# Layer 0 of a four-layer graph network: gathered rows in three bf16 parts, one-hot sums in bf16, gathers released four tiles at a time

## The chip, the cores and the metric

The kernel runs on one core of one Trainium2 chip. The metric is the device time of one run in microseconds (us), as the median of several runs. Besides the runs there is one execution under the hardware profiler, from which the page and the trace come.

## The reference

There are 8192 nodes with 32 features each and 262144 edges sorted by their target node `dst`. Four layers follow one another, and after each the node features are replaced by the layer norm of features plus layer output. The change concerns layer 0:

```python
w_e   = jnp.take(weight, etypes, axis=0)        # one of 64 matrices of 32x32 per edge
h_src = jnp.take(feat, src, axis=0)
msg   = jnp.einsum('ei,eio->eo', h_src, w_e)
out   = jax.ops.segment_sum(msg, dst, num_segments=8192)
```

Layer 1 sums `x[src] * edge_weight` over the edges of each target, layer 2 sums `x[src]`, and layer 3 makes a message from each edge's features with a small two-layer network and sums those.

## The kernel before

The edges stand in 2048 tiles (TT) of 128 edges, one edge per partition. Eight tiles (GT) make a group, so there are 256 groups (GG). Because the edges are sorted, the targets of one group fall into a window of 128 nodes; `rel` holds each edge's place in that window.

A first phase multiplies every node's features by all 64 matrices and writes the products to a table in DRAM, `ytab` (in the trace `fytab`), with 8192 x 64 rows of 32 numbers. The message of an edge is then one row of that table. While this phase runs, VectorE counts degrees and GpSimd fetches 64 records per node group, which `slots()` later turns into the tables `meta_l`, `meta_k` and `meta_w`.

The main loop of layer 0 does two independent things, interleaved in an order that is written out by hand. Each engine takes its own instructions strictly in the order of the program and waits only for the marks named in `after(...)`; `now(PE)` is the last mark that TensorE has been given so far.

The first thing is layer 0 itself. For group g:

- `gathers` (line 423) lets GpSimd issue one indirect DMA per tile (line 380 of the profile). It brings 128 rows of 32 f32 numbers from `ytab` into `xg`, which holds four slabs of 32 tiles. It is called once per slab of four groups. Before each group it waits until the sums that last read that place of `xg`, 16 groups back, are done (`taken`), and until the second last group of gathers has landed (`LAG`).
- `one_hot` (line 502) lets VectorE compare `rel` with an iota in PSUM, which gives an f32 matrix of 128 x 128 per tile in `oh` (four buffers).
- Eight f32 products on TensorE (line 605) sum the eight tiles into 32 columns of a PSUM bank; the profile shows each f32 product as two records. When 16 groups have filled a bank, ScalarE copies it to `win` (line 610).
- When enough of `win` is there, `windows` (line 492) shifts and adds the overlapping windows of eight node blocks on TensorE, and `normalize` (lines 451 to 461) does the layer norm on VectorE and ScalarE. This happens eight times.

The second thing is `matrices(i)`, 256 units that prepare layers 1 and 2. From group 8 on, group g is followed by one unit, sometimes by two. In a unit VectorE builds one-hot matrices (lines 554, 556, 559; `w_ps` in PSUM holds edge weights, refreshed by line 552), TensorE multiplies them in four quarters q0 to q3 of eight f32 products each (line 568), ScalarE evicts each quarter (lines 572 and 573), and SyncE stores 1 MB to `amat` and 0.5 MB to `cmat` (lines 577 and 578). VectorE's one-hot matrices have two buffers, so it starts unit i when q3 of unit i-2 is done.

Before group 4 the loop waits for `slots()`, whose transposes (line 530) run on TensorE and whose evictions (line 534) run on ScalarE.

Layer 1 begins when the last unit and the last normalization of layer 0 are done (line 643 loads `amat`). Layer 3 gathers too, from another table (`fxtab`), and there GpSimd is let go four tiles at a time, by the products of line 860.

Of the kernel before, what the change touches and what calls it, by code (L numbers as in the profile page):

```python
# [13 lines left out]
BF = mybir.dt.bfloat16  # L14
# [131 lines left out]
def raw_layers(tc, x, a, w0, w1, b1, w2, si, m, bad):  # L146
# [34 lines left out]
    def now(f):  # L181
        return (f.sem, f.n)
# [16 lines left out]
    st_c = cut(2, 4, 2, 256, dt=BF)  # L199

    xg = cut(4, WT, D)
    oh = cut(4, GT, P)
    win = cut(GG, D)
    end0 = cut.at

# [22 lines left out]
    hi_b = digits[:, 0:TT // 2].bitcast(BF)  # L228
    lo_b = digits[:, TT // 2:TT].bitcast(BF)
    iota = bank[:, 7, 0:P]  # L230
    w_ps = bank[:, 7, P:P + 384]


    dsti = rel.bitcast(I32)
# [210 lines left out]
    def normalize(l, c, acc, pm, x_in, x_out, x3=None):  # L445


        ds = slice(c * LC, (c + 1) * LC)
        y, yc, sq = (lnf[:, k].rearrange("p (d f) -> p d f", f=D) for k in range(3))
        V.after(pm, ln_last[0])  # L450
        read = own(V, V.e.tensor_add(y, acc.rearrange("p (d f) -> p d f", f=D), x_in[:, ds, :]))
        own(V, V.e.tensor_reduce(lns[:, 0], y, AX.X, OP.add))
        own(V, V.e.tensor_scalar(lns[:, 1], lns[:, 0], 1.0 / D, None, op0=OP.mult))
        vm = V.mark(V.e.tensor_sub(yc, y, lns[:, 1, :, None].to_broadcast([P, LC, D])))
        A.after(vm)
        V.after(A.mark(A.e.activation(sq, yc, AF.Square)))
        A.after(V.mark(V.e.tensor_reduce(lns[:, 2], sq, AX.X, OP.add)))
        V.after(A.mark(A.e.activation(lns[:, 0], lns[:, 2], AF.Sqrt, bias=eps, scale=1.0 / D)))
        own(V, V.e.reciprocal(lns[:, 3], lns[:, 0]))
        xo = x_out[:, ds, :]  # L460
        ln_last[0] = V.mark(V.e.tensor_tensor(xo, yc, lns[:, 3, :, None].to_broadcast([P, LC, D]), op=OP.mult))
        if x3 is not None:

            r1, r2 = y, sq
            V.after(ln_last[0])
            own(V, V.e.tensor_copy(x3[:, ds, 0:D], xo))
            own(V, V.e.tensor_sub(r1, xo, x3[:, ds, 0:D]))
            own(V, V.e.tensor_copy(x3[:, ds, D:2 * D], r1))
            own(V, V.e.tensor_sub(r2, r1, x3[:, ds, D:2 * D]))
            ln_last[0] = V.mark(V.e.tensor_copy(x3[:, ds, 2 * D:], r2))  # L470
        if l == 2:
            S.after(ln_last[0])
            x_st.add(S.e.dma_start(xtab.rearrange("(d p) f -> p d f", p=P)[:, ds, :], xo))
        return read

    def windows(c, acc, free):

        d0 = c * LC
        todo = []
        for j in [0, 1, 2, 3, -2, -1, 4]:  # L480
# [64 lines left out]
    def matrices(i):  # L545

        b, pp, k0 = i % 2, i // 2, 16 * (i % 2)
        WB = 24
        if i % WB == 0:
            n = min(WB * 16, CB * 16 - i * 16)  # L550
            V.after(now(V))
            own(V, V.e.tensor_copy(w_ps[:, 0:n], meta_w.rearrange("p n k -> p (n k)")[:, i * 16:i * 16 + n]))
        V.after(oh_used[b])
        own(V, V.e.tensor_tensor(oh_k[:, b, :, 0, :], iota[:, None, 0:64].to_broadcast([P, 16, 64]),  # L554
                                 meta_k[:, pp, k0:k0 + 16, None].to_broadcast([P, 16, 64]), op=OP.is_equal))
        V.e.tensor_tensor(oh_l[:, b], iota[:, None, :].to_broadcast([P, 16, P]),  # L556
                          meta_l[:, pp, k0:k0 + 16, None].to_broadcast([P, 16, P]), op=OP.is_equal)
        wo = (i % WB) * 16
        vm = V.mark(V.e.tensor_tensor(oh_k[:, b, :, 1, :], oh_k[:, b, :, 0, :],
                                      w_ps[:, wo:wo + 16, None].to_broadcast([P, 16, 64]), op=OP.mult))  # L560
        PE.after(vm)
        for q in range(4):
            bk = 3 + 2 * (units[0] % 2)
            PE.after(bank_free[units[0] % 2])
            for j in range(4):
                for h in range(2):
                    hs_ = slice(64 * h, 64 * h + 64)
                    ins = PE.e.matmul(bank[:, bk + h, :].rearrange("p (c s j) -> p c s j", s=64, j=4)[:, :, :, j],  # L568
                                      oh_l[hs_, b, 4 * q + j, :], oh_k[hs_, b, 4 * q + j], start=True, stop=True)
            pm = PE.mark(ins)  # L570
            A.after(pm, st_ld[b].mark() if q == 0 and st_ld[b].n else None)
            A.e.activation(st_c[:, b, q], bank[:, bk:bk + 2, 0:256], AF.Copy)  # L572
            bank_free[units[0] % 2] = am = A.mark(A.e.activation(st_a[:, b, q], bank[:, bk:bk + 2, 256:512], AF.Copy))  # L573
            units[0] += 1
        oh_used[b] = pm
        S.after(am)
        st_ld[b].add(S.e.dma_start(amat[:, 2048 * i:2048 * (i + 1)], st_a[:, b].rearrange("p u h c -> p (u h c)")))
        st_ld[b].add(S.e.dma_start(cmat[:, 2048 * i:2048 * (i + 1)], st_c[:, b].rearrange("p u h c -> p (u h c)")))
# [10 lines left out]
    FIRST = 8  # L589
    made = 0  # L590
    done = 0
    per = 512 // D
    for g in range(GG):
        s, h, bk, c = g * GT // WT, g % NO, (g // per) % 2, g % per
        if g == FIRST // 2:
            V.after(slots(), x_in)
        if g * GT % WT == 0:
            k, landed = gathers(ytab, row, s)
        V.after(oh_free[h])
        om = V.mark(one_hot(oh[:, h], g * GT, GT))  # L600
        PE.after(landed[g % 4], om)
        if c == 0:
            PE.after(agg_free[bk])
        for t in range(GT):
            ins = PE.e.matmul(bank[:, bk, c * D:(c + 1) * D], oh[:, h, t, :], xg[:, k, g * GT % WT + t, :],  # L605
                              start=(t == 0), stop=(t == GT - 1))
        oh_free[h] = taken[k][g % 4] = pm = PE.mark(ins)
        if c == per - 1:
            A.after(pm)
            agg_free[bk] = am = A.mark(A.e.activation(win[:, g + 1 - per:g + 1, :].rearrange("p g f -> p (g f)"),  # L610
                                                      bank[:, bk, :], AF.Copy))
            while done < NB // LC and ready(done) <= g + 1:
                pm = windows(done, bank[:, 2, 0:LC * D], (acc_free[0], am))
                acc_free[0] = normalize(0, done, bank[:, 2, 0:LC * D], pm, x_a, x_b)
                done += 1
        if g >= FIRST:
            upto = min(CB, (g - FIRST + 1) * CB // (GG - FIRST - 4))
            while made < upto:
                matrices(made)
                made += 1  # L620
    stored = [ld.mark() for ld in st_ld]


# [140 lines left out]
    def fetch_rows(q):  # L764

        if q < NQ:
            G.after(quad.get(q - AHEAD, {}).get("w"))
            rows[q // 8] = gathers(xtab, src, q // 8, q % 8 * 4, 4)
# [640 lines left out]
```

## Time and profile before

| | |
|---|---|
| median of 3 runs | 7803.98 us (7796.38 to 7807.71) |
| profiled execution | 7682.45 us, span 7680.7 us |
| TensorE busy (matmuls), weight loads | 76%, 55% of the span |
| VectorE, ScalarE, GpSimd busy | 49%, 22%, 52% |
| granted TensorE clock, mean | 0.792 |
| first phase | until about 272 us, where the gathers of layer 0 begin |
| layer 0's loop with units | 605 to 3593 us (first and last store of `amat`) |
| layers 1 and 2 | about 3611 to 4600 us |
| layer 3 | about 4600 to 7680 us |

The trace's times count from the span's start. In its rows a name left of `<-` is written, those right of it are read; `x8` means eight instructions merged into one row, and the brackets at the end give the engine's idle time just before and what is taken to have ended it. "remote" and "issue" are waits whose releaser the profile does not show. DMA-issuing time of SyncE stands under SPq.

### The profile page before, as it was taken

How to read it: one execution, taken by the hardware profiler on the slowest of the kernel's cores; microseconds unless marked ns; L12 is line 12 of the kernel's file. 1: busy time of each engine (PE TensorE's matmuls, PEld its weight loads, DVE VectorE, ACT ScalarE, POOL GpSimd, SP SyncE). 2: the span in 40 equal slices, each digit the busy share in tenths (PEclk: the TensorE clock that was granted, in tenths of full speed). 3: DMA queues.
4: the chain of work that ended last, by engine and by line, in shares of the span. 5: the costliest groups of instructions: out<-in, count | busy, mean ns of one | idle time of the engine just before them, and what ended most of it. 6: DMA issues, size and time to landing. Idle time of an engine off the chain costs nothing.

```text
span 7680.7 us, 88486 instructions
## 1 busy us (share of the span) xinstructions
PE 5868.9 (76%) x36084; PEld 4261.6 (55%) x36084; DVE 3758.9 (49%) x6691; ACT 1653.0 (22%) x2828; POOL 4001.1 (52%) x4174
## 2 busy tenths in 40 slices
PE   5327777787877778786444776989898889888898
PEld 2116767776767667676222344555555555555555
DVE  3304444444444454544000004666666766676666
ACT  3123333333333333333000001111111111111111
POOL 3456656565656656561000006666666666666663
PEclk7556777777777777777777887999999899999999
DMA  8405655555555555567999981111111111111111
GB/s 285 144 10 125 144 141 143 142 145 140 143 142 145 148 134 151 136 149 217 432 432 429 403 336 26 24 24 24 24 24 27 24 24 24 24 24 24 24 24 19
DMA packets 290736, 999.46 MB, mean 130 GB/s; under 512 B 99022, under 2 KB 175887, under 8 KB 250639
## 3 DMA queue, kind: packets, MB, share of 16 engines
q1 hardware_dynamic: 155742, 916.89, 33.0%
q0 software_dynamic: 134144, 73.67, 9.4%
q8 instruction: 286, 4.69, 0.3%
q10 hardware_dynamic: 432, 3.15, 0.1%
q14 instruction: 132, 1.07, 0.1%
HBM read 521.39 MB, written 471.99 MB: 129 GB/s over the span
## 4 chain that ended last, share of the span: by engine, by line
PE 51%; DVE 15%; another core or an unknown queue 15%; DMA 10%; issue 6%; ACT 3%; SPq 0%; DVEq 0%; ACTq 0%
PE bank L869 16%; PE bank L568 15%; PE bank L860 9%; DMA f_arena<-famat 6%; PE bank L605 3%; PE bank L836 3%; DMA f_arena<-fcmat 3%; DVE f_arena L904 3%; DVE f_arena L502 2%; DVE f_arena L556 2%; PE bank L684 2%; PE bank L687 2%; DVE f_arena L900 2%; ACT f_arena L573 1%
## 5 line engine op out<-in xcount | busy, mean ns | idle before, releaser
L380 POOL DMA_INDIRECT f_arena<-fxtab,f_src x2048 | 1971.8, 963 | 2135.8 <-DVE f_arena L740 1111.0
L380 POOL DMA_INDIRECT f_arena<-fytab,f_row x2048 | 1962.0, 958 | 1338.6 <-issue 552.8
L568 PE MATMUL bank<-f_arena 64*128 64x128 f32 x16384 | 1846.0, 376 | 580.1 <-issue 416.2
L568 PEld LDWEIGHTS bank<-f_arena 64*128 64x128 f32 x16384 | 1619.5, 275 | 792.3 <-issue 572.6
L869 PE MATMUL bank<-f_arena 128*128 128x344 f32 x4096 | 1486.7, 511 | 288.6 <-DVE f_arena L502 284.2
L869 PEld LDWEIGHTS bank<-f_arena 128*128 128x128 f32 x4096 | 860.2, 214 | 764.2 <-DVE f_arena L502 348.7
L572 ACT ACTIVATE f_arena<-bank 128x512 bf16<-128x512 f32 x1024 | 612.3, 598 | 1886.7 <-remote 1163.8
L860 PE MATMUL bank<-f_arena 65*128 65x256 f32 x4096 | 1005.2, 388 | 0.0
L554 DVE TENSOR_TENSOR f_arena<-bank,f_arena 128x1024 f32<-128x1024 f32 x256 | 313.3, 1224 | 1363.4 <-remote 1281.6
L860 PEld LDWEIGHTS bank<-f_arena 65*128 65x128 f32 x4096 | 762.5, 191 | 357.3 <-issue 223.0
L844 ACT ACTIVATE f_arena<-bank,f_arena 64x512 f32<-64x512 f32 x512 | 351.1, 686 | 2530.8 <-PE bank L836 909.5
L502 DVE TENSOR_TENSOR f_arena<-bank,f_rel 128x512 f32<-128x512 f32 (+1 forms) x768 | 659.1, 859 | 246.1 <-ACT f_arena L534 233.6
L605 PE MATMUL bank<-f_arena 128*128 128x32 f32 x4096 | 545.3, 283 | 125.4 <-DMA f_arena<-fytab,f_row 69.0
L573 ACT ACTIVATE f_arena<-bank 128x512 f32<-128x512 f32 x1024 | 607.7, 593 | 0.0
L605 PEld LDWEIGHTS bank<-f_arena 128*128 128x128 f32 x4096 | 509.8, 199 | 155.2 <-issue 107.3
L556 DVE TENSOR_TENSOR f_arena<-bank,f_arena 128x2048 f32<-128x2048 f32 x256 | 586.6, 2291 | 8.8
L904 DVE TENSOR_TENSOR f_arena<-bank,f_arena 128x256 f32<-128x256 f32 x1536 | 551.3, 415 | 0.0
L684 PE MATMUL bank<-f_arena,f_x_b 128*32 128x256 f32 x4096 | 293.9, 458 | 335.5 <-DMA f_arena<-famat 335.5
L897 DVE TENSOR_TENSOR f_arena<-bank,f_arena 128x256 f32<-128x256 f32 x512 | 215.9, 422 | 660.8 <-PE bank L860 288.0
L684 PEld LDWEIGHTS bank<-f_arena,f_x_b 128*32 128x32 f32 x4096 | 145.5, 131 | 472.6 <-DMA f_arena<-famat 309.8
L900 DVE TENSOR_TENSOR f_arena<-bank,f_arena 128x512 f32<-128x512 f32 x512 | 348.8, 681 | 0.0
L687 PE MATMUL bank<-f_arena 128*96 128x512 bf16 x1024 | 248.7, 405 | 80.1 <-DMA f_arena<-fcmat 80.1
(127 smaller groups left out, 2628.1 us busy)
## 6 DMA issues: line engine op xcount, KB each, us to landing
famat<-f_arena SPq DMA_DIRECT2D x256, 1024.0 KB
fcmat<-f_arena SPq DMA_DIRECT2D x256, 512.0 KB
fytab<-f_arena SPq DMA_DIRECT2D x64, 1024.0 KB
f_arena<-fytab,f_row POOLq DMA_INDIRECT x2048
f_arena<-fxtab,f_src POOLq DMA_INDIRECT x2048
f_arena<-laid_ea SPq DMA_DIRECT2D x64, 512.0 KB
f_arena<-laid_ea SPq DMA_DIRECT2D x64, 64.0 KB
f_arena<-laid_xT ACTq DMA_DIRECT2D x1, 1024.0 KB, 8.0
```

The costliest lines, as they stand in the source:

```text
L380: return G.e.indirect_dma_start(out=dest, out_offset=None, in_=table, in_offset=bass.IndirectOffsetOnAxis(ap=ix, axis=0))
L502: return V.e.tensor_tensor(o, iota[:, None, :].to_broadcast([P, n, P]), rel[:, t:t + n, None].to_broadcast([P, n, P]), op=OP.is_equal)
L556: V.e.tensor_tensor(oh_l[:, b], iota[:, None, :].to_broadcast([P, 16, P]), meta_l[:, pp, k0:k0 + 16, None].to_broadcast([P, 16, P]), op=OP ...
L568: ins = PE.e.matmul(bank[:, bk + h, :].rearrange("p (c s j) -> p c s j", s=64, j=4)[:, :, :, j], oh_l[hs_, b, 4 * q + j, :], oh_k[hs_, b, ...
L572: A.e.activation(st_c[:, b, q], bank[:, bk:bk + 2, 0:256], AF.Copy)
L573: bank_free[units[0] % 2] = am = A.mark(A.e.activation(st_a[:, b, q], bank[:, bk:bk + 2, 256:512], AF.Copy))
L605: ins = PE.e.matmul(bank[:, bk, c * D:(c + 1) * D], oh[:, h, t, :], xg[:, k, g * GT % WT + t, :], start=(t == 0), stop=(t == GT - 1))
L684: ins = PE.e.matmul(bank[q * D:(q + 1) * D, b, 0:256].rearrange("p (u h j) -> p u h j", h=2, j=4), x_b[:, s, :], mv[:, s], start=(s < 4), ...
L860: ins = PE.e.matmul(wp[:, t, :], hs[0:65, q % 4, t * P:(t + 1) * P], w2_s[0:65], start=True, stop=True)
L869: ins = PE.e.matmul(bank[:, g % 2, 0:MW], oh[:, c % NO, t, :], p[:, c % NP, t, :], start=(c % 2 == 0 and t == 0), stop=(c % 2 == 1 and t = ...
L900: V.e.tensor_tensor(pq[:, :, 0:128].rearrange("p t (o k) -> p t o k", k=16), wp[:, :, 0:128].rearrange("p t (o k) -> p t o k", k=16), a0[: ...
L904: V.e.tensor_tensor(pq[:, :, 128 + 64 * mm:192 + 64 * mm].rearrange("p t (o i) -> p t o i", i=8), wp[:, :, 192:256].rearrange("p t (o i) - ...
```

## The change

- The one-hot matrices `oh` are written in bf16.
- A new function `parts(g)` lets VectorE split the f32 rows of a group in three bf16 parts. It masks the upper 16 bits into PSUM (`x_ps`, which takes room from `w_ps`), converts them to bf16, subtracts, and does this again for the remainder. It is six instructions on 128 x 256 numbers. It waits for the landing of the group's gathers; `taken` is now marked by its first subtraction.
- TensorE multiplies each bf16 one-hot with the 96 columns of the three parts. A PSUM bank now takes four groups, and VectorE (`bank_out`) adds the three parts of each into `win`, two groups later than before; ScalarE's copy is gone.
- Gathers are issued in halves of four tiles by `fetch_rows`. Twelve groups are issued ahead of the loop. After that, the first half of group g+12 waits for the sums of group g, and the second half for the last TensorE mark after the units of group g.
- `w_ps` is refreshed every 8 units instead of every 24.

```diff
-    oh = cut(4, GT, P)
+    oh = cut(4, GT, P, dt=BF)
+    xp = cut(4, GT, 3, D, dt=BF)
+    xr = cut(2, GT * D)
...
-    w_ps = bank[:, 7, P:P + 384]
+    w_ps = bank[:, 7, P:2 * P]
+    x_ps = bank[:, 7, 2 * P:2 * P + GT * D]
...
-        WB = 24
+        WB = 8
...
+    def fetch_rows(g, h, let):
+        if g < GG:
+            G.after(let)
+            gathers(ytab, row, g * GT // WT, g * GT % WT + h * GT // 2, GT // 2)
+            if h == 1:
+                landed[g] = under_way[-1]
+    def parts(g):
+        k, t0, u = g * GT // WT % 4, g * GT % WT, g % 4
+        xv = xg[:, k, t0:t0 + GT, :].rearrange("p t f -> p (t f)")
+        r = xr[:, g % 2]
+        pi = x_ps.bitcast(I32)
...
+        V.after(landed[g], prev_parts[0])
+        own(V, V.e.tensor_scalar(pi, xv.bitcast(I32), upper16, None, op0=OP.bitwise_and))
+        V.e.tensor_copy(part[0], tf(x_ps))
+        taken[k][g % 4] = own(V, V.e.tensor_tensor(r, xv, x_ps, op=OP.subtract))
+        own(V, V.e.tensor_scalar(pi, r.bitcast(I32), upper16, None, op0=OP.bitwise_and))
+        V.e.tensor_copy(part[1], tf(x_ps))
+        prev_parts[0] = V.mark(V.e.tensor_tensor(part[2], tf(r), tf(x_ps), op=OP.subtract))
+        return prev_parts[0]
+    def bank_out(n):
+        V.after(sums_of[per * n + per - 1])
+        agg_free[n % 2] = vm = V.mark(V.e.tensor_reduce(
+            win[:, per * n:per * (n + 1), :], bank[:, n % 2, 0:per * 3 * D].rearrange("p (g c f) -> p g f c", c=3, f=D),
+            AX.X, OP.add))
+        return vm
...
+    for g in range(AHEAD):
+        for h in range(2):
+            fetch_rows(g, h, None)
+    for g in range(GG + 2):
+        if g >= 2 and (g - 2) % per == per - 1:
+            vm = bank_out((g - 2) // per)
+            while done < NB // LC and ready(done) <= g - 1:
...
-        if g * GT % WT == 0:
-            k, landed = gathers(ytab, row, s)
         V.after(oh_free[h])
-        om = V.mark(one_hot(oh[:, h], g * GT, GT))
-        PE.after(landed[g % 4], om)
+        one_hot(oh[:, h], g * GT, GT)
+        PE.after(parts(g))
...
-            ins = PE.e.matmul(bank[:, bk, c * D:(c + 1) * D], oh[:, h, t, :], xg[:, k, g * GT % WT + t, :],
-                              start=(t == 0), stop=(t == GT - 1))
-        oh_free[h] = taken[k][g % 4] = pm = PE.mark(ins)
-        if c == per - 1:
-            A.after(pm)
-            agg_free[bk] = am = A.mark(A.e.activation(win[:, g + 1 - per:g + 1, :].rearrange("p g f -> p (g f)"),
-                                                      bank[:, bk, :], AF.Copy))
...
+            ins = PE.e.matmul(bank[:, bk, 3 * c * D:3 * (c + 1) * D], oh[:, h, t, :],
+                              xp[:, g % 4, t].rearrange("p c f -> p (c f)"), start=(t == 0), stop=(t == GT - 1))
+        oh_free[h] = sums_of[g] = PE.mark(ins)
+        fetch_rows(g + AHEAD, 0, sums_of[g])
         if g >= FIRST:
...
                 matrices(made)
                 made += 1
+        fetch_rows(g + AHEAD, 1, now(PE))
```

More of the change, by code (lines that the diff above doesn't have):

```diff
@@ L591, in raw_layers @@
     done = 0
-    per = 512 // D
-    for g in range(GG):
-        s, h, bk, c = g * GT // WT, g % NO, (g // per) % 2, g % per
+    per = 4
+    AHEAD = 12
+    landed = {}
+    sums_of = {}
+    made_at = [None]
+    upper16 = -65536
+    def fetch_rows(g, h, let):
[9 more added lines that the diff above has]
+        pi = x_ps.bitcast(I32)
+        part = [xp[:, u, :, c, :] for c in range(3)]
+        tf = lambda v: v.rearrange("p (t f) -> p t f", f=D)
+        V.after(landed[g], prev_parts[0])
[6 more added lines that the diff above has]
+        return prev_parts[0]
@@ new lines, in bank_out @@
+    def bank_out(n):
[4 more added lines that the diff above has]
+        return vm
+    prev_parts = [None]
+    for g in range(AHEAD):
[5 more added lines that the diff above has]
+            while done < NB // LC and ready(done) <= g - 1:
+                pm = windows(done, bank[:, 2, 0:LC * D], (acc_free[0], vm))
+                acc_free[0] = normalize(0, done, bank[:, 2, 0:LC * D], pm, x_a, x_b)
+                done += 1
+        if g >= GG:
+            continue
+        h, bk, c = g % NO, (g // per) % 2, g % per
@@ L604, in raw_layers @@
         for t in range(GT):
-            ins = PE.e.matmul(bank[:, bk, c * D:(c + 1) * D], oh[:, h, t, :], xg[:, k, g * GT % WT + t, :],
-                              start=(t == 0), stop=(t == GT - 1))
-        oh_free[h] = taken[k][g % 4] = pm = PE.mark(ins)
-        if c == per - 1:
-            A.after(pm)
-            agg_free[bk] = am = A.mark(A.e.activation(win[:, g + 1 - per:g + 1, :].rearrange("p g f -> p (g f)"),
-                                                      bank[:, bk, :], AF.Copy))
[L612 to L615, printed above, removed]
+            ins = PE.e.matmul(bank[:, bk, 3 * c * D:3 * (c + 1) * D], oh[:, h, t, :],
+                              xp[:, g % 4, t].rearrange("p c f -> p (c f)"), start=(t == 0), stop=(t == GT - 1))
+        oh_free[h] = sums_of[g] = PE.mark(ins)
+        fetch_rows(g + AHEAD, 0, sums_of[g])
         if g >= FIRST:
```

## The prediction

> **What bounds the kernel now.** The page first: TensorE is the busiest engine, and the two gathers (L380) are the longest rows; the one into f_row's table (fytab) is layer 0's.
>
> ```profile
> PE 5868.9 (76%) x36084; PEld 4261.6 (55%) x36084; DVE 3758.9 (49%) x6691; ACT 1653.0 (22%) x2828; POOL 4001.1 (52%) x4174
> L380 POOL DMA_INDIRECT f_arena<-fytab,f_row x2048 | 1962.0, 958 | 1338.6 <-issue 552.8
> L568 PE MATMUL bank<-f_arena 64*128 64x128 f32 x16384 | 1846.0, 376 | 580.1 <-issue 416.2
> L605 PE MATMUL bank<-f_arena 128*128 128x32 f32 x4096 | 545.3, 283 | 125.4 <-DMA f_arena<-fytab,f_row 69.0
> ```
>
> The shares do not say what ends last, so next the stretches (columns: length, busy PE, PEld, DVE, ACT, POOL, granted clock, DMA share, GB/s). 605 to 3480 us is layer 0's main loop; from 3512 on its gathers are all done and the loop's last groups run without any.
>
> ```profile
> 605.00:3480.00 2875.00, 2260.98 (x19202) 2021.98 (x19201) 1392.32 (x1001) 1049.57 (x1954) 1740.00 (x1840) 0.72 0.57 143
> 3512.00:3590.00 78.00, 70.66 (x894) 66.55 (x892) 63.19 (x45) 47.33 (x92) 0.00 (x0) 0.93 0.75 226
> ```
>
> SyncE issues one amat store (L577) when a matrices unit is evicted, so its timeline is a clock of the loop:
>
> ```profile
> 2018.43 0.32 SPq L577 DMA_DIRECT2D famat<-f_arena  x1
> ...
> 2030.27 0.32 SPq L577 DMA_DIRECT2D famat<-f_arena  x1
> ```
> ```profile
> 3524.85 0.32 SPq L577 DMA_DIRECT2D famat<-f_arena  x1
> ...
> 3531.17 0.32 SPq L577 DMA_DIRECT2D famat<-f_arena  x1
> ```
>
> With gathers a group costs 11.8 us, without 6.32, for the same matmuls, evictions and stores. So TensorE's own work is not the bound. What stretches it is seen in the timelines of GpSimd, ScalarE and TensorE:
>
> ```profile
> 2017.72 0.95 POOL L380 DMA_INDIRECT f_arena<-fytab,f_row  x1 [2.11 <-remote]
> ...
> 2026.47 0.95 POOL L380 DMA_INDIRECT f_arena<-fytab,f_row  x1 [0.30 <-issue]
> 2029.55 0.95 POOL L380 DMA_INDIRECT f_arena<-fytab,f_row  x1 [2.13 <-remote]
> ```
> ```profile
> 2025.51 0.60 ACT L572 ACTIVATE f_arena<-bank 128x512 bf16<-128x512 f32 x1 [3.84 <-remote]
> ...
> 2029.15 0.60 ACT L572 ACTIVATE f_arena<-bank 128x512 bf16<-128x512 f32 x1 [2.56 <-remote]
> ```
> ```profile
> 2017.24 6.06 PE L568 MATMUL bank<-f_arena 64*128 64x128 f32 x56 [0.61 <-issue]
> ...
> 2023.23 2.19 PE L605 MATMUL bank<-f_arena 128*128 128x32 f32 x15
> ```
>
> Eight gathers go out 1.25 us apart (0.95 + 0.30). While they do, the signals of units q2 and q3 reach ScalarE only at 2025.51 and 2029.15, although their matmuls (and then the sums, L605) had started by 2023.3; the last comes 1.7 us after the last gather was built, and 0.4 us later GpSimd, which waits for the sums (L605) that follow q3, starts the next eight. It is a **lock-step**: gathers hold up TensorE's signals, and TensorE's signal lets the gathers go. A longer burst shows the price of one: 40 gathers from 543.24 to 592.04 kept the first eviction until 599.42:
>
> ```profile
> 519.60 18.37 ACT L534 ACTIVATE f_arena<-bank 128x512 bf16<-128x512 f32 x13 [1.81 <-PE bank L530]
> 599.42 0.60 ACT L572 ACTIVATE f_arena<-bank 128x512 bf16<-128x512 f32 x1 [61.45 <-remote]
> ```
>
> 56.2 us for 40 and 11.83 for 8 give 1.39 us a gather and 0.75 us for each hand-over. I do not know what resource this is.
>
> **The Trainium skill.** "SBUF — State Buffer", Who interferes with whom, says that PE and ACT never wait on anyone and that DMA never contends with a compute engine. The 11.8 against 6.32 disagree, at least for these gathers; the measurement decides. "TensorE: Matmul & The Clock Gate", its table of specifications, gives TensorE a queue of 64; that fits signals that come late while matmuls of later units have already started. The same page, Weight-path perf modes, says that weights of 128 columns that are not FP32 load about twice as fast; the trace agrees: a bf16 load of 128 columns (L318, first phase) takes 98 ns in the middle, L605's f32 loads 199 in the mean. "VectorE: DVE Perf Modes", Why PSUM operands drop a tier, leaves f32 operations with a PSUM operand at one element a cycle; the trace agrees: 415 and 422 ns for 256 elements (L904, L897), 561 for 384 (L552).
>
> **The change, part by part.** The profiled execution took 7682.45 us, 121.5 less than the median of the runs; I sum against the former and add 121.5.
>
> 1. *Sums on TensorE.* 8 f32 products (16 records, 1.86 us by the loads at 3529.94) become 8 bf16 records with 96 columns: at the f32 spacing of 0.116 us 0.95 us, at half of it 0.45. This saves 0.9 to 1.4 us of TensorE a group, all inside the lock-step, where TensorE has 5.5 us to spare: nothing by itself. It leaves more room in the queue for the next unit.
> 2. *Parts on VectorE.* Six operations of 256 elements, all with a PSUM operand, so 6 x 0.42 = 2.5, and about 0.15 for their own waits: 2.66 us a group (bounds 1.7 and 3.6). VectorE's group is now 1.22 (L502) + 4.83 (L554, L556, L559); with the parts, 1.05 units a group, a quarter of a 384-element reduce and w_ps in 32 pieces instead of 11 it comes to 9.1 us. Cover: the 11.8 us cycle. The one-hot and parts of group g+1 queue behind unit i, which starts two unit signals ahead; TensorE wants them a whole cycle later. Cost 0, except where no gathers run (item 6). bf16 one-hots read f32 from PSUM as before: 0.
> 3. *Release of the gathers.* GpSimd waited for the sums of 16 groups back. Now half a group waits for the sums of g and half for the last unit of g, 12 ahead. Sums follow the unit on TensorE at once, and both signals come as the burst drains (q3's eviction 2029.15, restart 2029.55), so I expect the second half of one group and the first of the next to go as one burst of eight, let go by q3 instead of the sums: 0.2 us sooner, times 231 cycles: **-46**. Behind it wait only gathers; the 2048 DMAs stay; SyncE's queue is not moved.
> 4. *Start.* 128 gathers instead of 160 run ahead of the transposes (L530), which crawl at 11.2 us a bank until the burst ends at about 519: the end comes 32 x 1.39 = 45 us sooner, of which VectorE's preparation of the slots, now behind parts(3) and its landing (338 instead of 308), costs 17. The burst of 40 before the first unit becomes 36: -7. Together **-35** (0 to -45).
> 5. *Twelve groups ahead.* 4.5 groups more pass through the cycle: 4.5 x 11.65 = **+52**.
> 6. *Tail.* Before, 119 us from the last gather (3492) to the end of layer 0's normalization (3611). After, 12 groups at VectorE's pace: 11 for the first, 7 x 9.1, 5 for a second unit, 4 x 3.9, 9.5 for the last windows: 105. **-14**.
> 7. *Windows.* ScalarE's L610 no longer stands ahead of them (5.5 us of idle TensorE), but one-hot and parts (3.9) now come between normalization and sums: 7 x -1.6 = **-11**. The 16 evictions L610 on ScalarE go; it is idle anyway.
>
> Sum: -54: 7628 profiled, **7750** median. Layers 1 to 3 are untouched.
>
> **Rivals.**
> *Two hand-overs (slower).* If the sums' signal is not out together with q3's but is held behind the half burst that q3 released, GpSimd stops twice a group and pays 0.75 twice: +0.75 x 231 without item 3, so -54 + 46 + 173 = +165 at the most, 7970; with half of the groups doing it, +80: 7880. It decides as soon as the sums' signal comes over 5 us after q3's, that is after four gathers. Against it: the 0.4 us above. For it: layer 3 releases by fours and pays 5.86 us per four (2980 us for 2035 gathers), hardly below 11.83 per eight.
> *Saturation.* If the lighter sums let q3 answer before the burst ends, GpSimd never stops: 8 x 1.39 = 11.1 a cycle, -54 + 46 - 168 = -176: 7630.
> *TensorE is the bound after all* (79% busy in the stretch): 1.1 x 244 = -270, 7530. The 6.32 us speak against it.
> *The halves change nothing* (the release does not do what it says): without items 3 and 4 the rest is +27, with one of them -19 or -8: about 7800.
>
> **How the numbers follow.** A measurement of this kernel can tell 0.2% (16 us) from no change. Forecast 0.36 (own range 7710 to 7785), saturation 0.11, TensorE 0.05: faster 0.52. Nothing 0.16. Two hand-overs 0.24, and 0.08 for VectorE operations or a gather service dearer than assumed: slower 0.32. The range 7640 to 7880 leaves out the ends of saturation and of the two hand-overs.
>
> **What would show it.** L577 issues 11.6 us apart in the middle of the loop; GpSimd in bursts of eight with one wait; VectorE's six new rows near 0.42 us; first L577 near 570 instead of 605; units about 9 us apart after the last gather. I am wrong if bursts of four with two waits show, if the cycle falls under 11 us, or if units wait for VectorE while gathers run.

## The result, and the profile after

The changed kernel takes 7687.32 us (median of 4, 7684.31 to 7698.31), the kernel before 7800.18 beside it (median of 4, 7794.36 to 7807.71). The ratio is 0.9862, interval 0.9845 to 0.9879: 113 us faster. The forecast was 7750 us, a gain of 54: the right direction, and less than half of the gain.

The profiled execution of the changed kernel took 7684.33 us, as long as its other runs. That of the kernel before took 7682.45, some 120 us less than its runs. Laid side by side the two profiles show no gain at all, and the experiments had to say which of them stands for what.

From the page of the changed kernel, the line of the engines and the gathers of layer 0:

```profile
PE 5356.7 (70%) x34036; PEld 3776.5 (49%) x34036; DVE 4365.5 (57%) x8312; ACT 1629.8 (21%) x2812; POOL 3983.9 (52%) x4174
L383 POOL DMA_INDIRECT f_arena<-fytab,f_row x2048 | 1957.6, 956 | 1344.5 <-issue 548.4
```

From its list of groups by line, the new sums (L657) and the first and last of VectorE's six operations (L619, L624):

```profile
L657 PE MATMUL bank<-f_arena 128*128 128x96 bf16 x2048 | 252.0, 253 | 320.7 <-issue 173.8 <-DVE f_arena L624 98.5 <-DVE bank L622 46.1
L619 DVE TENSOR_SCALAR bank<-f_arena 128x256 int32<-128x256 int32 x256 | 106.6, 416 | 29.8 <-DMA f_arena<-fytab,f_row 29.8
L624 DVE TENSOR_TENSOR f_arena<-f_arena,bank 128x256 bf16<-128x256 f32 x256 | 104.6, 409 | 0.0
```

TensorE lost 512 us of busy time and VectorE gained 607; GpSimd's time is nearly the same. The sums fell from 545.3 us (f32) to 252.0. The stretch of the loop (columns: length, busy PE, PEld, DVE, ACT, POOL, granted clock, DMA share, GB/s):

```profile
535.00:3480.00 2945.00, 1810.55 (x17654) 1605.91 (x17654) 1983.12 (x2511) 1045.15 (x1975) 1767.92 (x1873) 0.69 0.53 142
```

The first amat store comes at 534.57 us instead of 605.50. After that the loop keeps its cycle. SyncE's, GpSimd's and ScalarE's timelines in its middle:

```profile
2000.10 0.32 SPq L580 DMA_DIRECT2D famat<-f_arena  x1
...
2012.04 0.32 SPq L580 DMA_DIRECT2D famat<-f_arena  x1
```
```profile
2007.14 0.94 POOL L383 DMA_INDIRECT f_arena<-fytab,f_row  x1 [0.30 <-issue]
2010.34 0.94 POOL L383 DMA_INDIRECT f_arena<-fytab,f_row  x1 [2.26 <-PE bank L657]
```
```profile
2009.95 0.60 ACT L575 ACTIVATE f_arena<-bank 128x512 bf16<-128x512 f32 x1 [3.31 <-PE bank L571]
...
2010.92 0.60 ACT L575 ACTIVATE f_arena<-bank 128x512 bf16<-128x512 f32 x1
```

There are 11.94 us between these stores where the kernel before had 11.84, and bursts of eight gathers with one wait, as forecast. The wait is 2.26 us instead of 2.13. The bracket names the sums (L657), but all but a few of the bursts begin with the fifth gather of a group, and the program lets that one go by q3 of the unit before.

### The profile page after: what moved, and what is told of

The parts are those of the page before. It is cut to its first block, busy times and chain, and to the rows that moved or that the text cites. A ratio compares the mean times of both kernels' runs of the same rounds, so it can differ in the third digit from the quotient of the medians.

```text
span 7682.3 us, 85779 instructions
## 1 busy us (share of the span) xinstructions
PE 5356.7 (70%) x34036; PEld 3776.5 (49%) x34036; DVE 4365.5 (57%) x8312; ACT 1629.8 (21%) x2812; POOL 3983.9 (52%) x4174
## 3 DMA queue, kind: packets, MB, share of 16 engines
q1 hardware_dynamic: 155742, 916.89, 30.6%
## 4 chain that ended last, share of the span: by engine, by line
PE 53%; DVE 12%; another core or an unknown queue 11%; DMA 10%; issue 8%; ACT 6%; POOL 0%; SPq 0%; DVEq 0%; ACTq 0%; POOLq 0%
PE bank L571 18%; PE bank L915 17%; PE bank L906 9%; DMA f_arena<-famat 6%; PE bank L882 3%; ACT f_arena L576 3%; DMA f_arena<-fcmat 3%; DVE f_arena L950 2%; ACT f_arena L575 2%; PE bank L730 2%; DVE f_arena L505 2%; PE bank L733 2%; DVE f_arena L946 1%; PE bank L657 1%
## 5 line engine op out<-in xcount | busy, mean ns | idle before, releaser
L571 PE MATMUL bank<-f_arena 64*128 64x128 f32 x16384 | 1623.1, 374 | 959.3 <-issue 550.8
L571 PEld LDWEIGHTS bank<-f_arena 64*128 64x128 f32 x16384 | 1507.0, 279 | 1076.1 <-issue 899.3
L915 PEld LDWEIGHTS bank<-f_arena 128*128 128x128 f32 x4096 | 847.4, 211 | 790.4 <-DVE f_arena L505 364.0
L657 PE MATMUL bank<-f_arena 128*128 128x96 bf16 x2048 | 252.0, 253 | 320.7 <-issue 173.8
L657 PEld LDWEIGHTS bank<-f_arena 128*128 128x128 bf16 x2048 | 144.1, 118 | 413.3 <-issue 277.0
```

The lines of the kernel that those rows point to most:

```text
L657: ins = PE.e.matmul(bank[:, bk, 3 * c * D:3 * (c + 1) * D], oh[:, h, t, :], xp[:, g % 4, t].rearrange("p c f -> p (c f)"), start=(t == 0), ...
L915: ins = PE.e.matmul(bank[:, g % 2, 0:MW], oh[:, c % NO, t, :], p[:, c % NP, t, :], start=(c % 2 == 0 and t == 0), stop=(c % 2 == 1 and t = ...
```

## The experiments

The experiments ran in sets, each on one chip, whose number the results give, with the kernel before beside it. **Six sets ran on six chips, and the kernel before took very different times on them**: 7684.9 us on chip 10, 7761.3 on chip 13, and 6483.7, 6488.4, 6479.1 and 6479.7 on chips 4, 6, 0 and 14. That became the main finding. The sets follow chip by chip, in the order of their running but for the one on chip 14, which came last.

### Chip 10: where in the program the gain lies (before: 7684.88 us)

Both kernels with layer 3 cut short:

```
-    NQ = TT // 4
+    NQ = 24
+    NS = 3
```

> The kernel before with layer 3 cut to its first 24 of 512 quads (the rest of layer 3 is left out). In the profiled executions layer 3's first gather stood at 4603.4 us before and at 4564.2 after, so the 39 us gained in layer 0 were lost again in a layer 3 whose code is the same. Theory 'layer 0 holds it': in unprofiled runs the kernel before spends the 118 us that its profiled execution did not show in layer 0, so this kernel is about 113 us slower than the changed kernel cut in the same way (some 4770 profiled, 4880 unprofiled). Rival 'layer 3 wanders': layer 0 gives 39 us, and the rest is a layer 3 that runs at another rate from program to program; then the two cut kernels are 39 us apart, and this one's profiled and unprofiled times agree (4770).

> The changed kernel with layer 3 cut to its first 24 of 512 quads (the rest of layer 3 is left out). Theory 'layer 0 holds it': 113 us below the kernel before cut in the same way. Rival 'layer 3 wanders': 39 us below it. Both expect some 4730 us for this one, whose uncut form ran the same time profiled and unprofiled.

Measured: 4820.6 us for the kernel before (5 runs, 4812.11 to 4827.0) and 4721.58 for the changed one (4715.91 to 4723.64), 99.0 us apart. Ratios to the whole kernel before: 0.6278 (0.6269 to 0.6286) and 0.6145 (0.6137 to 0.6154). So a gain of 99 us lies ahead of layer 3; the whole changed kernel was not run on this chip. The half of the theory that said that the kernel before would be slow against its profile fell: on this chip it took 7684.88, just the time of its first profile. The two profiles of the first section therefore seem to belong to different levels (the level of a chip or an occasion is the time that the kernel before takes there): that of the kernel before matches a chip on which it runs 7685, that of the changed kernel the occasion on which the kernel before ran 7800. A difference read across them is worth nothing; these two, from one chip, can be compared.

Below, a signal of TensorE is called held when it comes clearly later than its matmul is over by the profile (whose ends of matmuls are modelled), and prompt when it comes at once. The evictions of the transposes on ScalarE, the last ones before the change and those after it:

```profile
494.96 2.39 ACT L534 ACTIVATE f_arena<-bank 128x512 bf16<-128x512 f32 x1 [8.81 <-remote]
504.76 2.39 ACT L534 ACTIVATE f_arena<-bank 128x512 bf16<-128x512 f32 x1 [7.41 <-remote]
512.46 2.39 ACT L534 ACTIVATE f_arena<-bank 128x512 bf16<-128x512 f32 x1 [5.32 <-remote]
515.28 9.43 ACT L534 ACTIVATE f_arena<-bank 128x512 bf16<-128x512 f32 x9 [0.43 <-remote]
```
```profile
344.91 29.39 ACT L537 ACTIVATE f_arena<-bank 128x512 bf16<-128x512 f32 x13 [86.61 <-PE bank L533]
...
458.27 1.02 ACT L537 ACTIVATE f_arena<-bank 128x512 f32<-128x512 f32 x1 [10.18 <-remote]
465.97 1.02 ACT L537 ACTIVATE f_arena<-bank 128x512 f32<-128x512 f32 x1 [6.68 <-remote]
469.49 1.88 ACT L537 ACTIVATE f_arena<-bank 128x512 f32<-128x512 f32 x2 [2.49 <-remote]
```

The first burst of gathers ends at 493.42 us before and at 455.55 after. After the change 13 of 24 banks are out before the hold begins, and when the burst ends 4 are left instead of 12. The first amat stores:

```profile
592.23 0.35 SPq L577 DMA_DIRECT2D famat<-f_arena  x1
```
```profile
532.45 0.35 SPq L580 DMA_DIRECT2D famat<-f_arena  x1
```

The milestones of the two timelines, in us:

| | before | after | difference | forecast |
|---|---|---|---|---|
| first amat store | 592.23 | 532.45 | -59.8 | -35 (item 4) |
| first store to last gather of layer 0 | 2883.4 | 2896.3 | +12.8 | -5 (items 3, 5, 7) |
| last gather to layer 3's first gather | 1117.1 | 1070.9 | -46.2 | -14 (item 6) |
| layer 3's first gather | 4592.78 | 4499.64 | -93.1 | -54 |

### Chip 10: each half of the change alone

The release alone is the kernel before with `fetch_rows` as in the change, PE's mark in both places, and its own f32 sums and evictions:

```
-        if g * GT % WT == 0:
-            k, landed = gathers(ytab, row, s)
...
         oh_free[h] = taken[k][g % 4] = pm = PE.mark(ins)
+        fetch_rows(g + AHEAD, 0, pm)
...
+        fetch_rows(g + AHEAD, 1, now(PE))
```

> The kernel before with only the release of the gathers changed (twelve groups ahead, half by half, the first half let go by the sums and the second by the last unit); f32 sums, ScalarE's eviction and the windows stay. Theory 'the release and the start hold it': ratio to before about 0.986 (7690 us). Rival 'the bf16 parts hold it': this gives the shorter start alone at most, 0.991 to 1.003. Items 3, 4 and 5 of the prediction by themselves sum to -29 us (0.996).

The parts alone are the changed kernel with the gathers issued as in the kernel before; their buffer still comes free at VectorE's first subtraction:

```
+        if g * GT % WT == 0:
+            for n, ld in enumerate(gathers(ytab, row, g * GT // WT)[1]):
+                landed[g + n] = ld
...
-        fetch_rows(g + AHEAD, 0, sums_of[g])
...
-        fetch_rows(g + AHEAD, 1, now(PE))
```

> The changed kernel with the release as before: a tile of 32 gathers at a time, limited only by the four buffers (16 groups ahead), and all else as changed (bf16 parts on VectorE, bf16 sums, eviction by VectorE). Theory 'the release and the start hold it': within 0.3% of before, ratio 0.997 to 1.005. Rival 'the bf16 parts hold it': about 0.986 to 0.990. The lock-step of the prediction expects the cycle of 11.8 us to stay.

Measured: the release alone 8241.99 us, ratio 1.0729 (1.0712 to 1.0747); the parts alone 8308.95, ratio 1.0814 (1.0796 to 1.0831). All expectations fell. **Each half by itself loses 7 to 8 per cent; together, in the cut kernels on the same chip, they gain 99 us.** The effects of the parts of this change cannot be added up.

Of the release alone, GpSimd's and ScalarE's timelines:

```profile
2011.62 0.94 POOL L380 DMA_INDIRECT f_arena<-fytab,f_row  x1 [0.31 <-issue]
2016.95 0.94 POOL L380 DMA_INDIRECT f_arena<-fytab,f_row  x1 [4.38 <-PE bank L568]
```
```profile
2008.45 0.60 ACT L572 ACTIVATE f_arena<-bank 128x512 bf16<-128x512 f32 x1 [4.71 <-PE bank L568]
...
2013.45 0.60 ACT L572 ACTIVATE f_arena<-bank 128x512 bf16<-128x512 f32 x1 [3.92 <-remote]
...
2014.42 0.60 ACT L572 ACTIVATE f_arena<-bank 128x512 bf16<-128x512 f32 x1
...
2016.71 0.60 ACT L572 ACTIVATE f_arena<-bank 128x512 bf16<-128x512 f32 x1 [1.20 <-PE bank L568]
```

There are eight gathers to a burst, as in the kernel before and nearly always in the changed one, but 4.4 us and more of wait after it (median 5.1, against 2.1 in both cut kernels). The burst is let go by q3 (L568); its first 3.3 us meet f32 sums on TensorE; of the next unit, q1 and q2 come out only when it is over (2013.45, 2014.42), and q3, which needs the bank of q1, is computed after that (2016.71). In the changed kernel the sums are short, and q3 is computed by about the time that the burst ends (2008.6 against 2008.1 us). That is a reading of the timelines; the kernel meant to test it met other conditions (below).

Of the parts alone, GpSimd's, ScalarE's and TensorE's timelines:

```profile
2032.07 0.94 POOL L383 DMA_INDIRECT f_arena<-fytab,f_row  x1 [11.50 <-DVE f_arena L621]
```
```profile
2016.92 0.60 ACT L575 ACTIVATE f_arena<-bank 128x512 bf16<-128x512 f32 x1 [16.52 <-remote]
```
```profile
2018.06 2.08 PE L571 MATMUL bank<-f_arena 64*128 64x128 f32 x16 [16.44 <-issue]
```

Here VectorE gives buffers back (L621) before TensorE has its sums, and GpSimd takes them at once: from 700 to 2400 us there are bursts of 24, 16 and 8, where the other kernels have only eights, or eights and some fours. In the burst from 1990.9 to 2020.6 us ScalarE got two signals of units, 17.6 us apart (q1's came 16.9 us after its matmul's end), and TensorE, which needs q1's bank evicted, stood for 16.4 us. That the early release makes the bursts long, and the bursts the loss, is again a reading of the timelines.

The two also split the start. First store of the release alone and of the parts alone:

```profile
561.62 0.35 SPq L577 DMA_DIRECT2D famat<-f_arena  x1
```
```profile
576.43 0.35 SPq L580 DMA_DIRECT2D famat<-f_arena  x1
```

Against 592.23 that is 30.6 us sooner with fewer gathers ahead and 15.8 with the parts, where the two together gave 59.8.

### Chips 4, 6, 0 and 14: signals that are not held (before: 6479 to 6488 us)

Four kernels were to settle this: the changed kernel again; the start alone, which is the kernel before with its fourth slab of 32 gathers held back until the slots are done; the release alone with whole groups let go by the sums; and the parts alone with the buffer coming free at the sums. The edits of the last three, against the kernel before, the release alone and the parts alone:

```
+            if s == 3:
+                G.after(drawn)
             k, landed = gathers(ytab, row, s)
```
```
         fetch_rows(g + AHEAD, 0, pm)
+        fetch_rows(g + AHEAD, 1, pm)
...
-        fetch_rows(g + AHEAD, 1, now(PE))
```
```
-        taken[k][g % 4] = own(V, V.e.tensor_tensor(r, xv, x_ps, op=OP.subtract))
+        own(V, V.e.tensor_tensor(r, xv, x_ps, op=OP.subtract))
...
-        oh_free[h] = sums_of[g] = PE.mark(ins)
+        oh_free[h] = sums_of[g] = taken[g * GT // WT % 4][g % 4] = PE.mark(ins)
```

(`drawn` is what `slots()` returns.)

> The changed kernel unaltered, timed again beside the kernel before. The kernel before ran 7685 us beside the first four experiments, 7800 beside the first timing of the change, and 7682 in its profiled execution; the two cut kernels were 99 us apart. Theory 'the place sets the level, the change gives about 100 us': the gain is there again, ratio 0.985 to 0.988, whatever level the kernel before has here. Rival 'the change only spares the kernel what it suffered in the first timing': where the kernel before runs 7685, this one runs 7685 too, ratio 0.998 to 1.002, and the 99 us of the cut kernels are made up by layer 3.

> The kernel before with one wait more: the gathers of the fourth tile of 32 wait for ScalarE's last eviction of the slots, so that 12 groups run ahead of the transposes instead of 16. All else as before. In the cut kernels the first amat store came 60 us sooner after the change (532.4 against 592.2), while the prediction had 35. Theory 'the start is most of the gain': 50 to 70 us gained, ratio 0.991 to 0.9935. Rival 'what starts sooner only waits longer later, since the gathers are the bound': 32 gathers late cost 32 x 1.25 = 40 us at the other end, ratio 0.997 to 1.003.

> The kernel before with twelve groups ahead, but whole groups let go by the sums (not half by half as in the release alone, which took 14.0 us a cycle and 8242 us). f32 sums stay. Theory 'the place of the burst on TensorE': let go by the sums, the burst begins together with unit q0 and two signals come through while it is young; let go by q3, its young part is spent on 3.6 us of f32 sums. So here the cycle is 11.8 us again and the time 7620 to 7700. Rival 'twelve groups ahead are too few for f32 sums': 8100 to 8250 as with the halves.

> The parts-alone kernel (8309 us) with one edit: a group's buffer comes free at the end of its sums on TensorE, not at VectorE's third part. Theory 'burst length': VectorE frees buffers early, GpSimd then runs 24 gathers in one burst, and TensorE's signals come out only after it; let go by the sums, the bursts are of eight again and the cycle 11.8 to 12 us, 7640 to 7740. Rival 'VectorE's six operations are themselves the price': 8200 to 8310 as before the edit.

Measured on chip 4, where the kernel before takes 6483.65 us: 1.0004 (0.9996 to 1.0013), 0.9998 (0.999 to 1.0007), 1.0003 (0.9995 to 1.0012) and 1.0003 (0.9995 to 1.0012). **The gain is gone, and so is every difference.** The expectations of this set were meant for held signals, which did not occur, so none of its theories was tested; the ratios near 1 that the first two rivals named came without their reason. The same four on another chip:

> The changed kernel unaltered, sent again with the three below, since in their first runs TensorE's signals were prompt (the kernel before took 6484 us, every kernel the same). Theory 'held signals': if the signals are held up here (the kernel before near 7700 or 7800), the gain of about 100 us is there, ratio 0.985 to 0.989; if they are prompt (6484), all four are at 0.999 to 1.001. Rival 'the gain was the first place's alone': held, but ratio 0.998 to 1.002.

> The kernel before with the gathers of the fourth tile of 32 waiting for the last eviction of the slots (12 groups ahead of the transposes instead of 16), sent again. Where signals are held: theory 'the start is most of the gain' 0.991 to 0.9935; rival 'what starts sooner waits later' 0.997 to 1.003. Where they are prompt: 1.000.

> The kernel before with twelve groups ahead, whole groups let go by the sums, f32 sums, sent again. Where signals are held: theory 'the place of the burst on TensorE' a cycle of 11.8 us, 0.989 to 1.002; rival 'twelve ahead are too few for f32 sums' 1.05 to 1.075. Where they are prompt: 1.000.

> The parts-alone kernel with the buffer coming free at the end of the sums, sent again. Where signals are held: theory 'burst length' 0.994 to 1.007; rival 'VectorE's six operations are the price' 1.065 to 1.08. Where they are prompt: 1.000.

Measured on chip 6 (before 6488.39 us): 1.0004 (0.9995 to 1.0012), 1.0003 (0.9994 to 1.0012), 1.0000 (0.9992 to 1.0009), 1.0004 (0.9996 to 1.0013), as expected for prompt signals. Two of them on a third chip:

> The kernel before with the gathers of the fourth tile of 32 waiting for the last eviction of the slots, and nothing else, once more, since its first two timings fell where signals were prompt. Where they are held (the kernel before near 7700 or 7800): theory 'the start is most of the gain' 0.991 to 0.9935, first amat store some 60 us sooner; rival 'what starts sooner waits later' 0.997 to 1.003. Where they are prompt: 1.000.

> The parts-alone kernel (1.081 where signals are held) with the buffer coming free at the end of the sums, once more. Where signals are held: theory 'burst length' 0.994 to 1.007 with bursts of eight; rival 'VectorE's six operations are the price' 1.065 to 1.08. Where they are prompt: 1.000.

Measured on chip 0 (before 6479.12 us): 0.9998 (0.9989 to 1.0007) and 1.0002 (0.9993 to 1.0011). And the same two on a fourth:

> The kernel before with the gathers of the fourth tile of 32 waiting for the last eviction of the slots, and nothing else, a fourth time (three fell where signals are prompt). Where they are held (the kernel before 7685 to 7800): theory 'the start is most of the gain' 0.991 to 0.9935, first amat store some 60 us sooner; rival 'what starts sooner waits later' 0.997 to 1.003. Where they are prompt: 1.000.

> The parts-alone kernel (1.081 where signals are held) with the buffer coming free at the end of the sums, a fourth time. Where signals are held: theory 'burst length' 0.994 to 1.007 with bursts of eight; rival 'VectorE's six operations are the price' 1.065 to 1.08. With half of the gathers VectorE's work was 9.2 us a group, below the 11.8 us of the cycle, which speaks for burst length. Where they are prompt: 1.000.

Measured on chip 14 (before 6479.74 us): 1.0001 (0.9992 to 1.001) and 1.0004 (0.9995 to 1.0012). The question that the last three of these kernels were made for stays open, since none of them met held signals. What the traces show instead is what bounds the loop here. A stretch of the loop on chip 4, the start alone (f32 sums) first, then the changed kernel, and GpSimd's timeline in the latter:

```profile
605.00:2780.00 2175.00, 1685.30 (x18158) 1591.25 (x18156) 1324.52 (x961) 970.03 (x1852) 1644.01 (x1743) 0.82 0.68 179
```
```profile
605.00:2780.00 2175.00, 1346.25 (x16382) 1245.55 (x16384) 1840.83 (x2340) 967.12 (x1831) 1644.73 (x1741) 0.81 0.68 179
```
```profile
1001.10 0.95 POOL L383 DMA_INDIRECT f_arena<-fytab,f_row  x1 [0.30 <-issue]
1002.35 0.94 POOL L383 DMA_INDIRECT f_arena<-fytab,f_row  x1 [0.30 <-issue]
```

The gathers come 1.25 us apart from end to end; GpSimd never waits: 2175 us for 1743 of them. TensorE's 1685 us in one and VectorE's 1841 in the other lie under that. The semaphore events of the traces say what differs from chip 10: from the end of a marked matmul to the next recorded signal the median is 0.02 us in the loop of the changed kernel here, and 1.09 in the kernel before and 1.13 in the changed one, both cut, where signals are held. (Where they are held the trace lacks part of these events, 303 of 2866 in the first profile of before against 10 in the start alone on chip 4, so these medians are rough.) Layer 3 gains as well: from first to last gather 2590 us here, 2996 in the first profile of before.

A chip that is slow in all things is excluded as the reason. Layers 1 and 2, which gather nothing, take 990 to 999 us from their first load to layer 3's first gather in all traces, prompt or held; the granted clock there is 0.77 to 0.78 in the first profile of before and on chips 10, 4 and 13. The stretches that differ all have gathers. The loop's granted clock, 0.72 in the kernel before on chip 10 and 0.82 in the start alone here, goes with TensorE's waits, and no run tells which follows from which.

### Chip 13: half of the gathers (before: 7761.25 us, signals held)

In both kernels every second gather of layer 0 is left out, and `xg` is set to zero beforehand, so that the rows that are not gathered are zero:

```
+            if t % every[0] == 0:
-            indirect(xg[:, k, t, :], table[:, :], ix[:, s * WT + t:s * WT + t + 1]).then_inc(ld.sem, 16)
-            ld.n += 16
+                indirect(xg[:, k, t, :], table[:, :], ix[:, s * WT + t:s * WT + t + 1]).then_inc(ld.sem, 16)
+                ld.n += 16
```

> The kernel before with every second gather of layer 0 left out (four per group instead of eight; the rows not gathered are zero), all else as before. Where signals are prompt, GpSimd's 1.26 us a gather is the bound; with half of them it needs 5.0 us a group, TensorE's own 6.3 us a unit takes over: 256 x 6.3 = 1610 us for a loop that took 2420, so some 5680 instead of 6484 (ratio 0.875). Where signals are held: 4 x 1.39 + 0.75 = 6.3 us a cycle instead of 11.8, at the least 6.3 from TensorE, so 6290 to 6500 instead of 7685. Rival 'something else than the gathers holds the prompt loop at 10.05 us a group': ratio over 0.97.

> The changed kernel with every second gather of layer 0 left out. The prediction costed the parts at nothing because VectorE's 9.1 us a group lay under a longer cycle. Theory 'hidden only by the gathers': with the cover gone, the loop takes 244 x 9.1 + some 60 = 2280 us where signals are prompt, 6340 in all, 11 to 12 per cent over the kernel before with half of its gathers; where they are held, some 6950. Rival 'the lighter sums make up for it': 0 to 3 per cent apart from the kernel before with half of its gathers, or below it.

Measured: the kernel before 6808.73 us, ratio 0.8777 (0.8753 to 0.8801); the changed one 6803.65, ratio 0.8763 (0.8738 to 0.8789). Signals were held, so 6290 to 6500 and 6950 were expected: both missed. The rival of the second expectation, 0 to 3 per cent between the two, came out in its number, though not by its reason, as follows. A stretch of each loop:

```profile
605.00:2580.00 1975.00, 1631.21 (x17987) 1509.05 (x17986) 1303.01 (x940) 972.44 (x1835) 812.39 (x863) 0.86 0.66 189
```
```profile
605.00:2580.00 1975.00, 1333.16 (x15943) 1194.49 (x15940) 1782.31 (x2271) 942.78 (x1784) 795.90 (x844) 0.83 0.65 185
```

With half of the gathers VectorE is busy 90% of the changed kernel's loop, 8.4 us for each of its 211 groups where the prediction summed 9.1 with waits, and the stores are 8.4 us apart (median): it is close to being the bound as soon as the gathers are fewer. The kernel before, with TensorE busy 83%, needs 8.7 (median), not 6.3. Its bursts are of four gathers with 4.0 us of wait after each (median), and a tenth of its signals still come about 2.6 us late or more. So the parts cost nothing against the kernel before even there, but because the latter does not reach its own floor; that held signals keep it from that floor was not tested. No experiment gave a version that beats both kernels.

## Why the prediction was right or wrong

**Right: the lock-step and the direction.** The cycle with its bursts of eight and one wait is there, the six operations take 0.41 to 0.43 us, and with all gathers VectorE's group is hidden under the cycle (item 2) in the changed kernel on every chip, at 67% busy in the loop where signals are held and 85% where they are prompt. TensorE's shorter sums (item 1) gave nothing by themselves where the gathers are prompt: 339 us less of busy TensorE than with f32 sums in the stretch on chip 4, and both kernels at the time of the kernel before. But the terms were summed as if each stood alone, and they do not: items 3, 4 and 5 by themselves give -29, and the release alone cost 557 us. That the direction came out although this dependence was not in the sum is in part luck.

**Item 4, the start, was mis-sized: -60, not -35.** The prediction took the end of the transposes from the end of the first burst, 45 us sooner, charged 17 us for VectorE's slots being later, and gave 7 us to the shorter burst behind them. The last term came (6 us). The end of the transposes went from 524.7 to 471.4 us, 53 sooner and not 28. The release alone moved it by only 25: its burst ends 40 us sooner, but then 19 banks are left instead of 12. The parts alone moved it by 28, sooner and not later, so the 17 had the wrong sign. Waiting behind the parts, the slots' VectorE work runs at 315 to 344 us (chip 10), while GpSimd's gathers take 6 to 8 us each; the transposes then start together with a fresh row of quick gathers, and 13 banks get out in 29 us before signals are held. In the kernel before they start 35 us into that row, and the first bank comes out at 360.56. What I missed was to ask how many banks would be left when the burst ends.

**Item 6, the tail, was mis-sized: -46, not -14.** Of the 46 us, 42 lie between the last gather and the first load of layer 1 (121.0 us before, 79.0 after, where 119 and 105 were forecast), and 4 in layers 1 and 2, which the change does not touch. I let the groups that were left cost VectorE's full 9.1 us. Nine units come in 61.5 us after the last gather, 6.8 each, where I had 80. VectorE is the bound, as forecast: in 45 us of it, on chip 10, it works for 44.28.

```profile
3435.00:3480.00 45.00, 30.14 (x424) 27.57 (x422) 44.28 (x55) 24.59 (x48) 0.00 (x0) 0.91 0.77 234
```

In those 61.5 us it makes the one-hots and parts of 8 groups, but the matrices of 7 units only: those of two units, 9.4 us of work, were ready before the last gather, and the sum had them in it. The rest of the difference is not broken down.

**Item 3, the release, failed as a mechanism.** It was right that q3 lets go a burst of eight: q3's signal comes at 2010.09 us and the gather 0.25 later. But the wait did not get shorter. Signals that were held come out in a row: q2 at 2009.93 and q3 at 2010.09, and the sums follow at 2010.22. Before, q3 at 2029.13 and the sums at 2029.29. Each kernel takes the second of its row, and the row starts when the burst is over. On chip 10 the wait is 2.11 us before and 2.09 after (medians), and the median distance of stores 11.80 and 11.76, so 0.04 us and not 0.2 a cycle.

**Item 7, the windows, erred the other way.** The mean distance of stores on chip 10 did fall by 0.2 us, from 11.95 to 11.75, but in its long intervals: those with windows take about 22 us before and 18 after, a gain of some 3.7 each where 1.6 was forecast, and most of the other long ones 13.5 and 12.6. So items 3 and 7 gave together some 43 us of the 57 forecast, most of it not where item 3 had it; that nearness is luck, and why the long intervals shrank by so much was not tested. Item 5 let 5 units more pass through the loop, about 59 us and not 52. With it the loop gives +12.8 where -5 was forecast, an error of 18 that hides part of those in items 4 and 6.

**The offset.** I took the 121.5 us between profile and median for a constant of the kernel and added them. Chip 10 suggests that they were two levels of the kernel before. On the level of its profile the forecast would have been 7628 of 7682, and the cut kernels say 99 us of gain there. The 14 us between 99 and 113 are not explained; there is no trace of the kernel before from the occasion on which it took 7800.

**The rivals.** "Two hand-overs" did not come: one wait follows eight gathers in 221 of 236 bursts on chip 10, and four in the others. A slower case did exist, and near: the release without the short sums waits 4.4 us a burst and loses 557 us. "Saturation" is what chips 4, 6, 0 and 14 have, but they have it in all kernels, through nothing that the change does. "TensorE is the bound" is excluded by those same chips, where TensorE does the same work in 10 us a group. "The halves change nothing" is excluded by the release alone: its bursts begin with the fifth gather of a group and are let go by q3, and it loses 7%.

## What to carry to other kernels

Before costing a change in a kernel whose parts wait for each other in turn, ask at which moment of the burst each released step starts: the same release lost 7% with f32 sums next in TensorE's queue and is part of a gain of 1.4% with short ones (that the sums' length is the reason is read from the timelines, not tested). Time a changed kernel beside the old one on several chips before trusting either a gain or a profile; here a gain of 1.4% on one was 0.0% on four others, and a profile taken apart from the timed runs hid it entirely. At a start, count how much work is left over when the burst that covers it ends, and not only when it ends.

## What the runs showed of the hardware that was not expected

Whether TensorE's completion signals come late while indirect gathers run depends on something outside the program. On two of the six chips, and in the first comparison to judge by its times, they do. On chip 10 they come a median of 1.1 us late in the kernel before and the changed one, and one came 16.9 us late in a burst of 24. Not every signal is late: in the parts alone, on the same chip, the median is 0.03 us, and a tenth are over 5.8 us late. On four chips signals come after 0.02 us, and the same kernel takes 6480 instead of 7685 to 7800 us. The recorded signals of ScalarE and VectorE come after 0.01 us (median) on chips 10 and 4 alike. Since the ends of matmuls are modelled, the traces do not tell a late signal from a matmul that ends late. The issue of one gather is the same in both, 0.94 us and 0.30 between. Each chip was used once, so the runs do not tell whether it is the chip or what else was there at the time. "SBUF — State Buffer" of the Trainium skill, Who interferes with whom, has TensorE waiting for nobody. That section is about the ports of SBUF, and no run here shows that a port is what is waited for. Taken as it stands, its sentence agrees with the traces of the four chips (0.02 us) and not with those of chip 10 (1.1 us).
